# Layer 2 attention in steps of three score tiles, values twelve tiles behind

## The chip, the cores and the metric

The kernel runs on one core of a Trainium2 chip, in one launch. The metric is the device time of an execution in microseconds (us). The engines are TensorE (PE; its weight loads are listed as PEld), VectorE (DVE), ScalarE (ACT), GpSimd (POOL) and SyncE (SP), which only starts DMAs here. Each engine runs its own instructions in order, and they wait for each other on semaphores.

## The reference, cut to what matters

Four layers of cross attention and feed-forward, each different, are added to `x` [4, 256, 256] in turn. The change lies in the attention of layer 2: 16 query heads in 4 groups that share keys and values, 1601 context tokens and the 256 tokens of `x` itself (causal), root-mean-square norms on q and k, rotary positions on q and on the keys of `x`.

```python
q = rms_norm((x @ wq).reshape(B, L, 16, 128), q_norm_w)
k = rms_norm((x @ wk).reshape(B, L, 4, 128), k_norm_w)
v = (x @ wv).reshape(B, L, 4, 128)
k_ctx = rms_norm((h_ctx_kv @ wk_ctx).reshape(B, T, 4, 128), k_norm_w)
v_ctx = (h_ctx_kv @ wv_ctx).reshape(B, T, 4, 128)
q = q * cos + rotate_half(q) * sin
k = k * cos + rotate_half(k) * sin
k_full = jnp.repeat(jnp.concatenate([k_ctx, k], axis=1), 4, axis=2)
v_full = jnp.repeat(jnp.concatenate([v_ctx, v], axis=1), 4, axis=2)
scores = jnp.einsum('blhd,bmhd->bhlm', q, k_full) / np.sqrt(128) + mask
out = jnp.einsum('bhlm,bmhd->blhd', jax.nn.softmax(scores, axis=-1), v_full)
return out.reshape(B, L, 2048) @ wo
...
x = x + _L2_xattn_ref(_layernorm(x, axis=-1), ctx_2048, ...)
x = x + _L2_ffn_ref(_layernorm(x, axis=-1), ...)
```

## The kernel before

Everything is float32. The keys and values of the context were made in an earlier stage and lie in DRAM. `l2_xattn` (L1349 to L1725) goes through 16 *units*: 4 batches times 4 groups of heads. A unit has 4 heads, a head 4 *score tiles*, so there are 256 tiles in all. A tile covers 64 of the 256 queries and all keys.

What happens to a head, with the lines:

- `scores` (L1549): for each of its 4 tiles, 8 matmuls of 128 x 32 weights write a tile `s` of two PSUM banks (pool `ps_s`, 3 buffers). Four of them use four column groups of the array side by side. Each matmul in float32 leaves two records in the trace. VectorE adds the mask (L1564) and takes the maximum (`nmsm`, L1567), ACT takes the exponential into `p` with its sum (L1572). The four 32-row groups of a tile hold different keys, so maxima and sums are partial.
- `merge` (L1581): the partial maxima and sums are brought together: copies on POOL, `lo`, `em`, `wm`, `tot` on VectorE, one exponential on ACT, `rm` on POOL (L1600). It is a generator with one break in it, after the exponential.
- `scale` (L1607): POOL multiplies `p` by the shares, 8 instructions a head. `turn` (L1613): VectorE transposes `p` into `pT`, 6 instructions a head.
- `values` (L1618): 15 matmuls a head over 15 key tiles, in four chunks (`CHUNK`: 4, 4, 4, 3), add up in `o`, a pool of **one** PSUM buffer (`ps_o`). Behind the last, ACT copies `o` to `at` (L1627), which makes `o` free for the next head.
- `project` (L1629): once a unit, 8 matmuls with `wo` into `acc`, added to `x` by VectorE.

Beside it `prep` (L1452), a generator too, makes the q, k and v of the next unit in pieces: `turned` (L1401; once a batch: layernorm of `x` and its transposes `tp_ln`), two halves of q (`tpq`, L1470 to L1490, with the square on ACT `sqq` L1477 and `ss`, `qo`, `qt` on VectorE L1478, L1480, L1482), k and v (`tpkv`), norms and rotary positions, then transposes of q (`tpqT`, L1526, twice) and k (`tpk`, L1531). All these and `acc` share one PSUM buffer (tag "tp", pool `ps`). The layernorm of batches 1 to 3 takes its root from an activation table on ACT; `exps_next` brings the exponential's table back. `self.root` is a Newton iteration on VectorE instead.

The order of the instructions: the Python loop issues two score tiles at a time (8 steps a unit); between them go the softmax of the head before (`softmax_steps`) and the values of the head before that (`value_steps`, two chunks a step, 8 tiles behind their scores); `WHEN` and `BETWEEN` say in which steps a piece of `prep` is issued. A scheduler then orders each engine's instructions by itself. What goes through `self.pin` keeps its place. `self.mm` (L116) pins a matmul only when `self.strict` is set, which it is not here.

Of the kernel before, what the change touches and what calls it, by code (L numbers as in the profile page):

```python
# [11 lines left out]
F32 = mybir.dt.float32  # L12
# [85 lines left out]
class Kernel:  # L98
# [1262 lines left out]
    def l2_xattn(self):  # L1361
# [10 lines left out]
        with ExitStack() as es:  # L1372
# [28 lines left out]
            def turned(b):  # L1401

                xn = self.xn.tile([P, 2, D], F32, name="xn")
                if b:
                    self.layernorm(xn, self.x[b])
                    exps_next()
                else:

                    mv = self.small.tile([P, 2, 2], F32, name="ln_mv")
                    for q in range(2):  # L1410
                        st = self.small.tile([P, 6], F32, name="st3")
                        nc.vector.bn_stats(st, self.x[b][:, q, :])
                        nc.vector.bn_aggr(mv[:, q, :], st)
                    r = self.small.tile([P, 8], F32, name="ln_r8", bufs=1)
                    self.root(r[:, :2], mv[:, :, 1], 1.0, 1e-5, r[:, 2:])
                    for q in range(2):
                        nc.vector.tensor_scalar(
                            xn[:, q, :], self.x[b][:, q, :], mv[:, q, 0:1], r[:, q : q + 1],
                            ALU.subtract, ALU.mult,
                        )  # L1420
                    self.fill(LN2)
                tp = ps.tile([P, 2, 2, P], F32, name="tp_ln", tag="tp")
                for k in range(2):
                    for q in range(2):
                        nc.tensor.transpose(tp[:, k, q, :], xn[:, q, k * P : (k + 1) * P], self.ident)
# [26 lines left out]
            def prep(u, w, res):  # L1452
# [3 lines left out]
                va = two.tile([P, NK, HD2], F32, name="va2", bufs=3)  # L1456
                kT = two.tile([P, NK, P], F32, name="kT2")
                kd, vd = self.early_kv[u]
                for t, d in ((kT, kd), (va, vd)):
                    nc.sync.dma_start(t[:, :CT, :], d[:, :CT, :])  # L1460
                nc.sync.dma_start(kT[:, CT, :96], kd[:, CT, :96])
                nc.sync.dma_start(va[:96, CT, :], vd[:96, CT, :])
# [4 lines left out]
                kr = one.tile([P, 2, HD2], F32, name="kr2")  # L1467
                ss = self.small.tile([P, 2 + 8], F32, name="ss2")
                ra, rb = tabs["l2_qnw"]
                qo = []  # L1470
                for q in range(2):
# [17 lines left out]
                    yield  # L1489
# [11 lines left out]
                yield  # L1501
# [8 lines left out]
                nc.vector.tensor_reduce(ss[:, :2], sq, AX.X, ALU.add)  # L1510
                self.rstd(ss, ss, 1.0 / HD2, self.eps6)
# [18 lines left out]
                for m in range(2):  # L1530
                    nc.tensor.transpose(tp[:, m, :], ko[:, m, :], self.ident)  # L1531
# [17 lines left out]
            def scores(kT, qT, h, c, ms):  # L1549
# [10 lines left out]
                p = main.tile([P, 2, NK * 32], F32, name="p2", bufs=8)  # L1560
# [79 lines left out]
            def softmax_steps(hd):  # L1640


                shares = merge(hd["ms"])
                next(shares)
                yield
                r = yield from shares
                hd["pT"] = main.tile([P, 8, NK, 32], F32, name="pT2")
                for c in range(4):
                    scale(hd["p"][c], r, c)
                yield  # L1650
                for c in range(4):
                    turn(hd["p"][c], hd["pT"], c)
                yield

            def value_steps(hd):
                o = ps_o.tile([P, S], F32, name="o2")
                for n, ms in enumerate(CHUNK):
                    values(hd["va"], hd["pT"], hd["at"], hd["h"], o, ms)
                    if n % 2:
                        yield  # L1660
# [7 lines left out]
            for _ in self.early:  # L1668
                pass
# [818 lines left out]
```

## Time and profile before

| | |
|---|---|
| median of 3 runs | 2395.33 us (2391.05 to 2395.61) |
| the profiled execution | 2387.69 us |
| its span | 2386.0 us |
| granted TensorE clock, mean | 0.973 |
| busy in the span: PE, DVE, ACT, POOL | 2255.6, 1473.2, 1272.4, 948.7 us |
| attention of layer 2, first score matmul | 691.07 us |
| its last projection | 1686.51 us, 3.05 us long |

The span is the time between the first and the last instruction that the profiler recorded; the profiled execution's time is 1.7 us longer. In a list of groups, each line gives line of code, engine and operation, output and input tiles, size, count, then busy us and the mean ns of one, then the engine's idle time just before and what ended most of it. Some groups of this stage:

```profile
L1572 ACT ACTIVATE p<-s,nmsm 128x448 f32<-128x448 f32 (+2 forms) x512 | 324.7, 639 | 369.6 <-DVE nmsm L1567 317.4
L117 PE MATMUL o<-pT,va 128*128 128x256 f32 (+2 forms) x1920 | 431.7, 377 | 3.3 <-DVE pT L1613 2.9
L117 PE MATMUL s<-kT,qT 128*32 128x448 f32 (+2 forms) x4096 | 424.2, 550 | 4.2 <-ACT p L1572 4.2
L1607 POOL TENSOR_SCALAR p<-p,rm 128x448 f32<-128x448 f32 (+2 forms) x512 | 320.7, 649 | 6.3
L1567 DVE TENSOR_REDUCE nmsm<-s 128x1 f32<-128x448 f32 (+4 forms) x384 | 293.2, 783 | 4.4
L1613 DVE STREAM_TRANSPOSE pT<-p 128x448 f32<-128x448 f32 (+4 forms) x384 | 278.1, 778 | 11.1 <-POOL p L1607 11.1
```

PE's o and s hold 431.7 and 424.2 us of the stage's 998, and had to wait for 3.3 and 4.2 us. ACT's exponentials sat idle for 369.6 us before them, most of it until VectorE's maxima.

### The profile page before, as it was taken

To read this page: it belongs to the slowest core of one execution; us is meant where nothing else is said; L and a number is where in the kernel's file an instruction comes from. 1 tells how busy PE (TensorE), PEld (TensorE's weight loads), DVE (VectorE), ACT (ScalarE), POOL (GpSimd) and SP (SyncE) were. 2 spreads that over 40 slices of the span, in tenths; PEclk is the share of its full clock that TensorE was granted. 3 is DMA by queue.
4 is the path that set the end of the run, shared out by engine and by line. 5 is a ranking of instruction groups with operands and counts; after the bars stand their busy time and mean duration, and the time that the engine had idled before them with its cause. 6 is when DMAs were issued, how large, how long until landed. Compare 5 with 4: busy or idle time off the path is not lost.

```text
span 2386.0 us, 42230 instructions
## 1 busy us (share of the span) xinstructions
PE 2255.6 (95%) x14335; PEld 1382.2 (58%) x14335; DVE 1473.2 (62%) x3553; ACT 1272.4 (53%) x2877; POOL 948.7 (40%) x1707
## 2 busy tenths in 40 slices
PE   8989997889989999999999999999899889999996
PEld 5677875777745555555555655555665533444332
DVE  5453532773457777777777777777334574758344
ACT  3334443552474555555555555553232577888994
POOL 1014655503335544555554555554121253334220
PEclk9989998989999999999999999999899999999998
DMA  7165575652550111111111111100534353434320
GB/s 267 41 201 161 172 156 157 197 185 65 167 179 32 43 51 47 47 51 51 51 52 51 51 51 50 44 10 10 205 124 117 114 156 103 109 94 103 83 64 19
DMA packets 156078, 234.47 MB, mean 98 GB/s; under 512 B 33929, under 2 KB 122761, under 8 KB 154666
## 3 DMA queue, kind: packets, MB, share of 16 engines
q1 hardware_dynamic: 138998, 190.07, 25.0%
q0 software_dynamic: 11280, 31.60, 5.4%
q10 hardware_dynamic: 5588, 10.09, 1.4%
q8 instruction: 117, 1.92, 0.3%
q14 instruction: 95, 0.78, 0.1%
HBM read 169.94 MB, written 61.74 MB: 97 GB/s over the span
## 4 chain that ended last, share of the span: by engine, by line
PE 78%; DVE 7%; issue 5%; DMA 4%; ACT 2%; POOL 2%; SPq 1%; ACTq 0%; POOLq 0%; DVEq 0%
PE o L117 17%; PE s L117 17%; PE o L77 6%; PE b L77 3%; PE f2gu L117 3%; PE s L77 3%; PE f1gu L117 2%; PE fill L1307 2%; PE f0gu L117 2%; PE acc L117 2%; PE tpq L117 2%; PE av L117 2%; PE f0y L117 2%; PE f2y L117 1%; PE f1y L117 1%
## 5 line engine op out<-in xcount | busy, mean ns | idle before, releaser
L1572 ACT ACTIVATE p<-s,nmsm 128x448 f32<-128x448 f32 (+2 forms) x512 | 324.7, 639 | 369.6 <-DVE nmsm L1567 317.4
L117 PE MATMUL o<-pT,va 128*128 128x256 f32 (+2 forms) x1920 | 431.7, 377 | 3.3 <-DVE pT L1613 2.9
L117 PE MATMUL s<-kT,qT 128*32 128x448 f32 (+2 forms) x4096 | 424.2, 550 | 4.2 <-ACT p L1572 4.2
L77 ACT ACTIVATE e<-s 128x1024 f32<-128x1024 f32 (+1 forms) x416 | 392.4, 1041 | 57.4 <-PE s L77 56.3
L117 PEld LDWEIGHTS o<-pT,va 128*128 128x128 f32 (+1 forms) x1920 | 344.7, 190 | 127.9 <-issue 75.4
L1607 POOL TENSOR_SCALAR p<-p,rm 128x448 f32<-128x448 f32 (+2 forms) x512 | 320.7, 649 | 6.3
L1567 DVE TENSOR_REDUCE nmsm<-s 128x1 f32<-128x448 f32 (+4 forms) x384 | 293.2, 783 | 4.4
L1613 DVE STREAM_TRANSPOSE pT<-p 128x448 f32<-128x448 f32 (+4 forms) x384 | 278.1, 778 | 11.1 <-POOL p L1607 11.1
L117 PEld LDWEIGHTS s<-kT,qT 128*32 128x32 f32 x4096 | 121.7, 109 | 250.2 <-issue 213.9
L77 PE MATMUL o<-e,va 128*32 128x512 f32 x1656 | 246.9, 614 | 12.3 <-DVE os L77 12.2
L1600 POOL TENSOR_TENSOR rm<-em,tot 32x8 f32<-32x8 f32 x256 | 50.3, 197 | 335.6 <-DVE tot L1597 303.3
L1564 DVE TENSOR_TENSOR s<-s,mask 128x64 f32<-128x64 f32 (+4 forms) x384 | 92.5, 260 | 128.5 <-PE s L117 82.4
L77 PEld LDWEIGHTS s<-qb,kb 32*128 32x128 f32 (+1 forms) x1664 | 65.5, 180 | 182.3 <-issue 143.7
L1307 PE MATMUL fill<-wkc_early,ctxT 128*128 128x256 f32 (+1 forms) x444 | 110.5, 401 | 8.9 <-ACT va_early L1315 6.7
L522 POOL DMA_INDIRECT f0xr<-f0xd,f0src x95 | 91.3, 961 | 66.5 <-PE f0y L117 25.5
L77 PE MATMUL s<-qb,kb 32*128 32x256 f32 (+1 forms) x1664 | 111.5, 331 | 3.1 <-ACT e L77 1.8
L77 POOL CAST kb<-kf 128x384 fp32r<-128x384 f32 (+1 forms) x126 | 65.5, 549 | 96.4 <-PE s L77 61.8
L1307 PEld LDWEIGHTS fill<-wkc_early,ctxT 128*128 128x128 f32 (+1 forms) x444 | 87.0, 200 | 25.3 <-ACT va_early L1315 7.8
L1572 ACT ACTIVATION_READ_ACCUMULATOR p<-s,nmsm 128x1 f32 x512 | 100.5, 196 | 0.0
L1326 DVE TENSOR_REDUCE ss_early<-sq_early 128x4 f32<-128x512 f32 x64 | 37.1, 580 | 82.8 <-ACT sq_early L1325 72.0
L630 POOL DMA_INDIRECT f0yt<-f0yd,f0slot x64 | 63.1, 987 | 60.7 <-DVE x L622 29.8
L117 PE MATMUL f2gu<-f2wgu,f2xsT 128*128 x176 | 85.1, 608 | 0.6 <-ACT f2xsT L114 0.3
(579 smaller groups left out, 3689.2 us busy)
## 6 DMA issues: line engine op xcount, KB each, us to landing
kf<-kd SPq DMA_DIRECT2D x384, 48.0 KB
vd<-va_early SPq DMA_DIRECT2D x96, 128.0 KB
kd<-kT_early SPq DMA_DIRECT2D x48, 256.0 KB
kT<-kd SPq DMA_DIRECT2D x16, 768.0 KB
va<-vd SPq DMA_DIRECT2D x16, 768.0 KB
kd<-kt SPq DMA_DIRECT2D x96, 128.0 KB
f0yd<-f0ys SPq DMA_DIRECT2D x95, 128.0 KB
ctxT<-in_ctxT SPq DMA_DIRECT2D x5, 1664.0 KB
```

What stands on the lines that cost most here:

```text
L77: ins = f(*a, **kw)
L117: self.ordered(self.nc.tensor.matmul(out, lhsT, rhs, start=start, stop=stop, **kw))
L522: nc.gpsimd.indirect_dma_start(out=t, out_offset=None, in_=xd[:, :], in_offset=bass.IndirectOffsetOnAxis(ap=src[:, n : n + 1], axis=0),)
L630: nc.gpsimd.indirect_dma_start(out=yt, out_offset=None, in_=yd[:, :], in_offset=bass.IndirectOffsetOnAxis(ap=slot[:, t, r : r + 1], axis=0),)
L1307: ins = nc.tensor.matmul(tp[:rows, t, :], ctxT[u // NKV2][:, k, c0 : c0 + rows], w[u % NKV2][:, k, :], start=k == 0, stop=k == 1,)
L1326: nc.vector.tensor_reduce(ss[:, m0:m1], sq[:, : m1 - m0, :], AX.X, ALU.add)
L1564: nc.vector.tensor_tensor(sv, sv, mask[:, e0:e1, : nt - CT, :].rearrange("p n t i -> p n (t i)"), ALU.add)
L1567: nc.vector.tensor_reduce(ms[:, 0, e0:e1], s[:, n0:n1, : nt * 32], AX.X, ALU.max, negate=True)
L1572: nc.scalar.activation(p[:, n, : nt * 32], s[:, n, : nt * 32], AF.Exp, bias=ms[:, 0, e : e + 1], accum_out=ms[:, 1, e : e + 1],)
L1600: nc.gpsimd.tensor_tensor(r[32 * a : 32 * a + 32], e[:, a], tot, ALU.mult)
L1607: nc.gpsimd.tensor_scalar(p[:, n, : nt * 32], p[:, n, : nt * 32], r[:, e : e + 1], 1.0, ALU.mult, ALU.mult)
L1613: self.pin(nc.vector.transpose(pT[:, 2 * c + n0 : 2 * c + n1, :nt, :].rearrange("p n t i -> p n (t i)"), p[:, n0:n1, : nt * 32],))
```

## The change

Tiles are numbered through all units: tile x belongs to head x // 4, to unit x // 16, and has place k = x % 16 in it.

- A step has three score tiles, issued one after the other, instead of two (`scores` returns `s`; mask, maximum and exponential are in `weights`, which is issued by `soften`).
- Values run `LATE` = 12 tiles behind: in the step of tiles x to x + 2, chunks of the tiles x - 12 to x - 10 (one chunk a tile).
- A head's merge and scaling come one step after its last tile, its transposes another step later. The ring of `p` has 12 buffers instead of 8.
- `self.strict` is set over the loop, and the transposes on PE go through `ordered`: PE runs the matmuls in the order in which they are written.
- `beside` places the pieces of `prep`, the loads and the projection by k. A unit's first pieces are made two units ahead of it. In `prep` the order is now: first half of q; loads of k and v, and `tpkv`; second half of q; norms.
- The layernorm in `turned` takes Newton's root for every batch.

```diff
@@ -1401,28 +1401,23 @@
             def turned(b):
...
-                if b:
-                    self.layernorm(xn, self.x[b])
-                    exps_next()
-                else:
...
+                r = self.small.tile([P, 8], F32, name="ln_r8", bufs=1)
+                self.root(r[:, :2], mv[:, :, 1], 1.0, 1e-5, r[:, 2:])
+                if b == 0:
                     self.fill(LN2)
...
-                        nc.tensor.transpose(tp[:, k, q, :], xn[:, q, k * P : (k + 1) * P], self.ident)
+                        self.ordered(nc.tensor.transpose(tp[:, k, q, :], xn[:, q, k * P : (k + 1) * P], self.ident))
@@ -1453,22 +1448,15 @@
-                va = two.tile([P, NK, HD2], F32, name="va2", bufs=3)
-                kT = two.tile([P, NK, P], F32, name="kT2")
-                kd, vd = self.early_kv[u]
-                for t, d in ((kT, kd), (va, vd)):
-                    nc.sync.dma_start(t[:, :CT, :], d[:, :CT, :])
-                nc.sync.dma_start(kT[:, CT, :96], kd[:, CT, :96])
-                nc.sync.dma_start(va[:96, CT, :], vd[:96, CT, :])
                 if u % NKV2 == 0:
                     self.xb = turned(b)
                     yield
                 xb = self.xb
-                kr = one.tile([P, 2, HD2], F32, name="kr2")
                 ss = self.small.tile([P, 2 + 8], F32, name="ss2")
-                ra, rb = tabs["l2_qnw"]
                 qo = []
-                for q in range(2):
+                def query(q):
+                    ra, rb = tabs["l2_qnw"]
...
-                    yield
+                query(0)
+                yield
+                va = two.tile([P, NK, HD2], F32, name="va2", bufs=3)
+                kT = two.tile([P, NK, P], F32, name="kT2")
+                kd, vd = self.early_kv[u]
+                for t, d in ((kT, kd), (va, vd)):
+                    nc.sync.dma_start(t[:, :CT, :], d[:, :CT, :])
+                nc.sync.dma_start(kT[:, CT, :96], kd[:, CT, :96])
+                nc.sync.dma_start(va[:96, CT, :], vd[:96, CT, :])
+                kr = one.tile([P, 2, HD2], F32, name="kr2")
                 tp = ps.tile([P, 2, 256], F32, name="tpkv", tag="tp")
...
-                yield
...
                 sq = one.tile([P, 2, HD2], F32, name="sq2")
                 nc.scalar.activation(sq, kr, AF.Square)
                 nc.vector.tensor_reduce(ss[:, :2], sq, AX.X, ALU.add)
+                yield
+                query(1)
+                yield
                 self.rstd(ss, ss, 1.0 / HD2, self.eps6)
                 exps_next()
...
-                    nc.tensor.transpose(tp[:, m, :], ko[:, m, :], self.ident)
+                    self.ordered(nc.tensor.transpose(tp[:, m, :], ko[:, m, :], self.ident))
...
-            def scores(kT, qT, h, c, ms):
...
-                p = main.tile([P, 2, NK * 32], F32, name="p2", bufs=8)
+                return s
+            def weights(s, c, ms):
+                p = main.tile([P, 2, NK * 32], F32, name="p2", bufs=12)
                 for n0, n1, nt in spans(c):
...
+            def value_chunk(hd, n):
+                if n == 0:
+                    hd["o"] = ps_o.tile([P, S], F32, name="o2")
+                values(hd["va"], hd["pT"], hd["at"], hd["h"], hd["o"], CHUNK[n])
 
             units = [(b, g) for b in range(B) for g in range(NKV2)]
             w = load(0)
             wo = load_out(0)
+            results = {0: []}
+            for n, _ in enumerate(prep(0, w, results[0])):
                 self.fill(Q2 if n == 0 else C2 if n == 3 else 0)
             for _ in self.early:
                 pass
+            w = load(1)
             self.es2.close()
             main = es.enter_context(tc.tile_pool(name="a2main", bufs=2, side="right", reuse_waits="tile"))
 
 
+            heads, pieces = [], {}
+            def begin(n):
+                for _ in pieces[n] if n else ():
+                    pass
+                kT, va, qT = results[n]
                 at = main.tile([P, 4, S], F32, name="at2", bufs=2)
                 for h in range(4):
+                    heads.append({"kT": kT, "va": va, "qT": qT, "at": at, "h": h, "b": units[n][0], "wo": wo, "p": []})
+            def prepare(n):
+                if n < len(units):
+                    if n not in pieces:
+                        pieces[n] = prep(n, w, results.setdefault(n, []))
+                    next(pieces[n], None)
+            def beside(n, k):
+                nonlocal w, wo
+                if k == 11 and n:
+                    project(heads[4 * n - 1])
+                if k in (1, 3, 7, 9) or (n, k) == (0, 0):
+                    prepare(n + 1)
+                if k == 12:
+                    for _ in range(2):
+                        prepare(n + 1)
+                    if n + 1 < len(units):
+                        wo = load_out(units[n + 1][1])
+                if k == 3 and n + 2 < len(units):
+                    w = load(units[n + 2][1])
+                if k == 15 or (k == 13 and (n + 2) % NKV2 == 0):
+                    prepare(n + 2)
+            def turns(hd):
+                hd["pT"] = main.tile([P, 8, NK, 32], F32, name="pT2")
+                for c in range(4):
+                    turn(hd["p"][c], hd["pT"], c)
+            def soften(made):
+                for hd, c, s in made:
+                    hd["p"].append(weights(s, c, hd["ms"]))
+            self.strict = True
+            merging, turning = [], []
+            LATE, ALL = 12, 16 * len(units)
+            for x0 in range(0, ALL + LATE, 3):
+                made, norms = [], False
+                for x in range(x0, min(x0 + 3, ALL)):
+                    if x % 16 == 0:
+                        begin(x // 16)
+                    hd = heads[x // 4]
+                    if x % 4 == 0:
+                        hd["ms"] = self.small.tile([P, 2, 8], F32, name="nmsm2")
+                    made.append((hd, x % 4, scores(hd["kT"], hd["qT"], hd["h"], x % 4)))
+                soften(made[:1])
+                merges = [(hd, merge(hd["ms"])) for hd in merging]
+                for _, steps in merges:
+                    next(steps)
+                soften(made[1:2])
+                for hd, steps in merges:
+                    try:
+                        next(steps)
+                    except StopIteration as end:
+                        for c in range(4):
+                            scale(hd["p"][c], end.value, c)
+                for pos in range(3):
+                    x = x0 + pos
+                    if LATE <= x < ALL + LATE:
+                        value_chunk(heads[(x - LATE) // 4], (x - LATE) % 4)
+                    if pos == 0:
+                        soften(made[2:])
+                    if x < ALL:
+                        beside(x // 16, x % 16)
+                        norms |= x % 16 == 4
+                    if pos == 0:
+                        for hd in turning:
+                            turns(hd)
+                if norms:
+                    prepare(x0 // 16 + 1)
+                turning, merging = merging, [hd for hd, c, _ in made if c == 3]
+            project(heads[-1])
+            self.strict = False
```

The old loop, which the new one replaces, is in the functions printed above (`softmax_steps`, `value_steps`, `WHEN`, `BETWEEN`).

## Prediction

> **What bounds the kernel now.** First the page's busy time and chain, to see which engine and which stage.
>
> ```profile
> PE 2255.6 (95%) x14335; PEld 1382.2 (58%) x14335; DVE 1473.2 (62%) x3553; ACT 1272.4 (53%) x2877; POOL 948.7 (40%) x1707
> ...
> PE 78%; DVE 7%; issue 5%; DMA 4%; ACT 2%; POOL 2%; SPq 1%; ACTq 0%; POOLq 0%; DVEq 0%
> PE o L117 17%; PE s L117 17%; PE o L77 6%; PE b L77 3%; PE f2gu L117 3%; PE s L77 3%; PE f1gu L117 2%; PE fill L1307 2%; PE f0gu L117 2%; PE acc L117 2%; PE tpq L117 2%; PE av L117 2%; PE f0y L117 2%; PE f2y L117 1%; PE f1y L117 1%
> ```
>
> TensorE sets the end, and the two largest entries (s and o, L117, 17% each) are the stage that is changed. Its first score matmul starts at 691.07 us and its last projection ends near 1689.6. Three windows of that stage (start and end, length, then busy us with instructions of PE, PEld, DVE, ACT, POOL, then granted clock, DMA share, GB/s) and PE's waits in it:
>
> ```profile
> 700.00:720.00 20.00, 15.78 (x121) 5.35 (x113) 17.68 (x41) 15.03 (x41) 10.60 (x24) 0.91 0.09 33
> 719.00:1659.00 940.00, 939.22 (x6348) 550.32 (x6348) 727.18 (x1577) 487.62 (x1359) 483.80 (x1076) 1.00 0.13 44
> 1660.00:1680.00 20.00, 17.66 (x96) 12.95 (x94) 13.85 (x27) 4.17 (x14) 12.33 (x28) 1.00 0.00 0
> ```
>
> ```profile
> PE s L117 <- ACT p L1572: 4.2, 3, 2.6
> PE o L117 <- DVE pT L1613: 0.3, 1, 0.3
> ```
>
> PE is busy for 939.22 of 940 us at full clock: nothing is waited for, so only what PE itself spends can be saved there. The waits lie in the start (4.2) and the end. Busy is not useful, though. A timeline of PE around two changes of kind (start, length, records of each run) shows it:
>
> ```profile
> 1016.93 0.99 PE L117 MATMUL s<-kT,qT 128*32 128x480 f32 x8
> ...
> 1017.33 0.59 PE L117 MATMUL s<-kT,qT 128*32 128x480 f32 x4
> 1017.84 0.48 PE L117 MATMUL o<-pT,va 128*128 128x256 f32 x1
> ...
> 1018.16 0.59 PE L117 MATMUL o<-pT,va 128*128 128x256 f32 x2
> ...
> 1039.71 0.27 PE L1526 MATMUL tpqT<-ident,qo 128*128 128x128 f32 x1
> 1040.02 0.48 PE L117 MATMUL o<-pT,va 128*128 128x256 f32 x1
> ```
>
> Four score records go side by side, a set every 0.40 us (1016.93 to 1017.33). From the last set to the first value record it is 1017.84 less 1017.35 (start of the set's fourth record) = 0.496 where the records of a set take 0.382 from there to the next set: +0.114. That first record lasts until 1018.16, 0.320, where later ones are 0.216 apart: +0.104. Into a score run, 0.309 follows the last record instead of 0.216, +0.094, and the first set is 0.024 longer. One score run costs 0.336 us of turnover. From transposes to values it is 0.306 instead of 0.109 (1039.71 to 1040.02) and again 0.104: 0.301. From values to q products, k/v products, projection or transposes it is nothing.
>
> **The change part by part.** *Steps of three tiles.* In the issue order of the two builds PE has 126 score runs before and 86 after. Before: 126 entries x 0.118, 111 exits to values x 0.218, 15 exits to q transposes x (0.114 + 0.060), 15 times transposes to values x 0.301: 14.9 + 24.2 + 2.6 + 4.5 = 46.2. After: 86 x 0.118 + 86 x 0.218 + 30 transposes to values x 0.301 (the pieces now stand among values, not before scores): 10.1 + 18.7 + 9.0 = 37.9. **-8.3 us**. The 38 joints from q, k/v and projection products to values do not occur before; nearest is values to the same products, 0, at most the transposes' 0.301: 0 to 11. I take 0, since shape and width are those of values.
>
> One rule speaks against this gain: the Trainium skill, "TensorE: Matmul & The Clock Gate", Part 2, says that PE loads weights ahead of matmuls in flight. By that a change of kind would be free and this term 0, the total 8.3 later; the 0.496 and 0.320 above differ, and the rows decide.
>
> *PE's order is pinned, values twelve tiles behind.* PSUM has one bank for o. The last chunk of a head must be copied (L1627) before the next head's first value matmul. Before, the two were parted: the copy ended 0.82 to 0.93 after the last record's start and the next head began 2.55 to 5.55 later still. After, the two chunks follow in one step if the last falls on its position 0 or 1, with only a piece between: q products (1.72 us), projection (1.3 before it needs that copy), or, at the unit's tile 7, four transposes (0.64). The bare copy:
>
> ```profile
> 1680.22 6.45 PE L117 MATMUL o<-pT,va 128*128 128x256 f32 x30 [2.54 <-DVE pT L1613]
> 1686.51 3.05 PE L117 MATMUL acc<-wo,at 128*128 128x256 f32 x12
> ...
> 1686.71 0.37 ACT L1627 COPY at<-o 128x256 f32<-128x256 f32 x1 [9.48 <-PE o L117]
> ```
>
> Uncovered it costs 0.379 (a record) + 0.04 + 0.37 - 0.216 = 0.57. Tile 7's 0.64 would hide just that, but ACT is in order, and in the built order that copy stands behind an exponential of the same step's tiles, which needs VectorE's maximum. A step is some 9.8 us of PE (3 x 1.65 scores, 22.5 x 0.216 values), 10.5 to 13.4 with a piece. VectorE averages 727.18 / 940 = 77%, but is uneven: six transposes (4.3 us) fall in one step with a query half (ss 0.69, qo 0.68, qt 0.68) that waits for ACT's square (0.60). By these rows I walked the 16 steps that repeat every three units:
> - Units 3, 6, 9, 12 (tile 7 at position 1): VectorE's transposes end 3.8 us into the step, the copy's exponentials follow, the copy ends 9.5 to 9.9 in; PE wants the bank at 8.65. 1.3 us each, times 4: 5.2.
> - Units 2, 5, 8, 11, 14 (position 0): behind the k sum of squares, three transposes and the query half, the copy ends 8.3 to 8.7 in, wanted at 6.85. 1.9 us each, times 5: 9.5.
> - Elsewhere the walk leaves 0.3 us or more.
> **+14.7**. Bounds: 0 if VectorE is 1.9 us earlier than walked; 9 x 3.0 = 27, where 3.0 is its fullest step, 12.8, less 9.8. I take the walk. Queued behind the waiting PE are only its own values and next scores; the wait gives VectorE time, so nothing is late after it.
> The last unit has no pieces: five bare handoffs x 0.6, **+3.0** (2.1 to 4.7).
>
> *Start and end.* The 2.54 idle before 1680.22 was VectorE's last turns. After, head 63's chain of merge, scaling and turns is some 16.2 us against 17.3 of values still to do: **-2.5** (0 to -2.5). At the start the first values come after 15 tiles instead of about 11 and fewer pieces fill PE: idle 4 to 6 instead of 4.2, and a q product (1.72) that stood in it moves out: **+1** (-4 to +5).
>
> *At no cost.* Newton roots for batches 1 to 3: fewer ACT table loads, some ten small VectorE operations each; PE waited for neither before, and the result is wanted a step later. If VectorE has no slack there, some 1.5 us three times. The k and v loads go behind a query, some 15 tiles (50 us) ahead of use, at 0.13 DMA share; the query weights a unit ahead. SP's order behind them stays. The larger weights ring (8 to 12) only takes waits away.
>
> **Sum.** -8.3 + 14.7 + 3.0 - 2.5 + 1 = +7.9. On the profiled execution's 2387.69 that is 2395.6; the median of the runs is 2395.33, 7.6 above it, so I forecast the median + 7.9 = **2403**.
>
> **The rivals.** *The cover holds (faster):* the copies come before PE wants the bank, at tile 7 of nine units. For it: VectorE idles 23% on average, and one us of walk error clears half. Against: in order it cannot use that idle time early. Decides when the copy ends within 6.85 and 8.65 us of the step's start: -8.3 + 3.0 - 2.5 + 1 = -6.8, 2388.5; with no bare handoffs either 2385.5.
> *Half of it:* one of the two kinds of unit stalls: -6.8 + 5.2 or 9.5, 2394 to 2398, not told from before.
> *The throttle joins:* after the start's idle 2.60 us the clock in the first window was 0.91: (1 - 0.91) x 20 = 1.8 us lost; after 2.54 idle in the third it stayed 1.00. If each of nine stalls were followed by that: 9 x 1.8 = 16, 2419. Against it, each stall is shorter than either.
> The same page's Part 1 gives an idle window of about 3.4 us before the clock is halved; by it this rival is 0, though 2.60 us was enough (with 0.91 and 0.70 shortly before) in the first window.
> *Scores wait for their buffers:* three tiles fill the ring of three; a tile's exponential has about 4.9 us of values as cover. If VectorE's uneven steps break that too, +0.5 us in 30 steps, 2418.
>
> **How the numbers follow.** Forecast 0.42 (its own range 2397 to 2412, mostly the stalls' 8 to 24), cover holds 0.25, half 0.15, throttle or buffers 0.18. This kernel's times differ by 0.2% between runs, so same is 2390.5 to 2400.1. Faster: 0.25. Same: the half and the forecast's lowest 0.05, 0.20. Slower: 0.37 + 0.18 = 0.55. The range leaves out a tenth at each end: 2385 to 2421.
>
> **What would show it.** Right: PE busy falls by some 8 us in the middle windows at clock 1.00, and PE o waits for ACT's at copy 14 times, some 18 us in sum, the nine at tile 7 the longest; the idle before the tail's values is gone. Wrong: waits at those nine absent (cover holds); score waits on p (buffers); clock under 1.00 after stalls; or a last set to first value record no longer 0.496, or products to values not 0.216.

## The result and the profile after

The changed kernel takes 2412.55 us (median of 4 runs, 2410.57 to 2415.17), the kernel before 2395.40 (4 runs): a ratio of 1.0077, with a 95% interval of 1.0059 to 1.0094. That is 17 us slower. Its profiled execution took 2415.17 us, its span is 2413.5.

Busy time of the engines on the page, and the stage in three windows (start and end; length; busy us of PE, PEld, DVE, ACT, POOL with instructions; granted clock, DMA share, GB/s). The windows go from the first score matmul to tile 48, from there to tile 192, and on to the last projection. The kernel before, cut at the same tiles:

```profile
691.00:867.00 176.00, 171.70 (x1175) 94.97 (x1174) 135.41 (x293) 95.95 (x267) 89.71 (x201) 0.99 0.14 50
867.00:1427.00 560.00, 559.39 (x3780) 328.27 (x3782) 433.98 (x941) 294.15 (x812) 288.72 (x639) 1.00 0.14 49
1427.00:1690.00 263.00, 259.87 (x1722) 155.84 (x1714) 193.74 (x420) 123.08 (x345) 128.10 (x288) 1.00 0.08 28
```

And the changed kernel:

```profile
PE 2249.5 (93%) x14322; PEld 1389.0 (58%) x14335; DVE 1506.1 (62%) x3586; ACT 1267.4 (53%) x2871; POOL 950.4 (39%) x1707
...
701.00:887.00 186.00, 170.31 (x1157) 92.44 (x1156) 138.85 (x293) 95.95 (x267) 90.51 (x197) 0.97 0.16 53
887.00:1448.00 561.00, 552.19 (x3772) 330.25 (x3770) 445.12 (x937) 290.98 (x809) 290.54 (x640) 1.00 0.15 49
1448.00:1713.00 265.00, 259.85 (x1749) 160.76 (x1748) 202.45 (x425) 122.23 (x346) 129.53 (x293) 1.00 0.08 26
```

PE's busy time fell by 6 us over the span, and by 7.2 in the middle window (559.39 to 552.19), where the kernel before was idle for only 0.6 us: the longer runs do save work. But the middle window is no shorter, and the first is 10 us longer. To the hundredth, from the times of the tiles' first score records: the first 48 tiles take 186.35 us instead of 176.14, the next 144 take 560.61 instead of 559.46, and the stage, to the start of the last projection's last record, 1011.75 instead of 998.12. PE's waits in the stage of the changed kernel (total, times, longest):

```profile
PE o L117 <- ACT at L1631: 13.0, 15, 1.6
PE tpkv L117 <- issue: 5.2, 2, 4.3
PE acc L117 <- ACT at L1631: 3.2, 4, 0.8
PE s L117 <- ACT p L1576: 2.6, 3, 1.4
PE tpqT L1526 <- POOL qo L1516: 2.4, 1, 2.4
PE tpk L1531 <- DVE x L1639: 1.9, 1, 1.9
PE o L117 <- DVE pT L1617: 1.0, 1, 1.0
```

Three things stand here.

*The single o bank.* Of the 15 waits for the copy, five are at tile 7 in position 0 (1.19 to 1.58 us), four at tile 7 in position 1 (0.81 each), five are the bare ones of the last unit (0.46 to 0.52), one is in the start. Timelines of VectorE, ACT and PE of the changed kernel, in this order, at one of the first kind show why (start, length, engine, line, tiles, records):

```profile
1039.35 3.19 DVE L1617 STREAM_TRANSPOSE pT<-p 128x896 f32<-128x896 f32 x4
1042.48 0.42 DVE L1568 TENSOR_TENSOR s<-s,mask 128x192 f32<-128x192 f32 x2
```

```profile
1044.09 0.66 ACT L1576 ACTIVATE p<-s,nmsm 128x480 f32<-128x480 f32 x1 [5.08 <-DVE nmsm L1571]
...
1044.74 0.65 ACT L1576 ACTIVATE p<-s,nmsm 128x480 f32<-128x480 f32 x1
...
1045.38 0.60 ACT L1576 ACTIVATE p<-s,nmsm 128x416 f32<-128x416 f32 x1
...
1045.96 0.38 ACT L1631 COPY at<-o 128x256 f32<-128x256 f32 x1
```

```profile
1042.81 1.56 PE L117 MATMUL o<-pT,va 128*128 128x256 f32 x6
1044.20 0.60 PE L1526 MATMUL tpqT<-ident,qo 128*128 128x128 f32 x4
1046.38 0.48 PE L117 MATMUL o<-pT,va 128*128 128x256 f32 x1 [1.58 <-ACT at L1631]
```

The last chunk is done near 1044.4, and ACT has been idle for 5.08 us just before. But VectorE was at its transposes until 1042.48 and its masks and maxima come after; the exponentials wait for these, and the copy stands behind three of them.

*The start.* Timelines of PE and of VectorE of the changed kernel:

```profile
706.72 1.98 PE L117 MATMUL tpq<-wq,xT 128*128 128x512 f32 x4
713.01 3.38 PE L117 MATMUL tpkv<-wks,xT 128*128 128x256 f32 x8 [4.30 <-issue]
```

```profile
710.46 0.66 DVE L1571 TENSOR_REDUCE nmsm<-s 128x1 f32<-128x480 f32 x1
711.04 0.67 DVE L1466 TENSOR_REDUCE ss<-sqq 128x4 f32<-128x512 f32 x1
711.63 0.68 DVE L1468 TENSOR_TENSOR qo<-tpq,l_qnwra 128x512 f32<-128x512 f32 x1
712.23 0.68 DVE L1470 TENSOR_TENSOR qt<-tpq,l_qnwrb 128x512 f32<-128x512 f32 x1
```

The k and v products need the buffer that the query half has just filled. The view names no releaser, but by the times VectorE reads that buffer last: it does so only after the masks and maxima of three tiles, until 712.9, and PE, in pinned order, may not take the next scores meanwhile.

*Before the stage.* The first score matmul comes 74.9 us after the start of the last expert matmul of the layer before it (626.2 to 701.06), where it was 71.5 (619.5 to 691.07). The experiments find the reason.

### The profile page after: what moved, and what is told of

The parts are those of the page before. It is cut to its first block, busy times and chain, and to the rows that moved or that the text cites. A ratio compares the mean times of both kernels' runs of the same rounds, so it can differ in the third digit from the quotient of the medians.

```text
span 2413.5 us, 42181 instructions
## 1 busy us (share of the span) xinstructions
PE 2249.5 (93%) x14322; PEld 1389.0 (58%) x14335; DVE 1506.1 (62%) x3586; ACT 1267.4 (53%) x2871; POOL 950.4 (39%) x1707
## 4 chain that ended last, share of the span: by engine, by line
PE 65%; DVE 18%; ACT 6%; issue 6%; DMA 2%; POOL 2%; SPq 0%; another core or an unknown queue 0%; ACTq 0%; PEld 0%; POOLq 0%; DVEq 0%; PEldq 0%
PE o L117 11%; PE s L117 10%; PE o L77 7%; DVE pT L1617 4%; PE b L77 3%; DVE nmsm L1571 3%; PE f2gu L117 3%; ACT p L1576 3%; PE s L77 3%; PE f1gu L117 2%; PE f0gu L117 2%; PE fill L1307 2%; PE acc L117 2%; PE av L117 2%; PE f0y L117 2%
## 5 line engine op out<-in xcount | busy, mean ns | idle before, releaser
L117 PE MATMUL s<-kT,qT 128*32 128x448 f32 (+2 forms) x4096 | 414.3, 552 | 2.6 <-ACT p L1576 2.6
L1571 DVE TENSOR_REDUCE nmsm<-s 128x1 f32<-128x448 f32 (+4 forms) x384 | 298.8, 785 | 7.4 <-DVE s L1568 0.2
L77 PE MATMUL o<-e,va 128*32 128x512 f32 x1656 | 248.0, 617 | 14.1 <-DVE os L77 12.2
L1326 DVE TENSOR_REDUCE ss_early<-sq_early 128x4 f32<-128x512 f32 x64 | 37.2, 581 | 85.0 <-ACT sq_early L1325 65.4
```

The costliest lines, as they stand in the source:

```text
L77: ins = f(*a, **kw)
L117: self.ordered(self.nc.tensor.matmul(out, lhsT, rhs, start=start, stop=stop, **kw))
L1326: nc.vector.tensor_reduce(ss[:, m0:m1], sq[:, : m1 - m0, :], AX.X, ALU.add)
L1571: nc.vector.tensor_reduce(ms[:, 0, e0:e1], s[:, n0:n1, : nt * 32], AX.X, ALU.max, negate=True)
```

## The experiments

The stage is counted from the first score matmul to the start of the last projection record in the run's profile, the stretch before it from the start of the last expert matmul of layer 1. "The 48 tiles" and "the steady tiles" are the first 48 score tiles and the 144 behind them, as in the windows above. The first four kernels ran on a chip on which the kernel before took 2343.0; ratios compare. The intervals are 95%. Stage and stretch come from one profiled execution each. Behind the stage the code is the same in all kernels, and yet these executions take from 695.0 us (e3) to 703.5 (e6) there, so a median need not show all of a gain in the stage.

| kernel | median us | before | ratio | stage us | stretch before |
|---|---|---|---|---|---|
| before (profile shown) | | | | 998.1 | 71.5 |
| changed kernel (profile shown) | 2412.55 | 2395.40 | 1.0077 (1.0059 to 1.0094) | 1011.8 | 74.9 |
| e1 two halves of the bank | 2364.37 | 2343.03 | 1.0081 (1.0053 to 1.0109) | 1013.6 | 73.6 |
| e2 steps of two | 2352.97 | 2343.03 | 1.0046 (1.0032 to 1.0059) | 1000.8 | 72.8 |
| e3 first loads early | 2364.72 | 2343.03 | 1.0087 (1.0059 to 1.0116) | 1015.0 | 72.9 |
| e4 start's pieces spread | 2360.77 | 2343.03 | 1.0075 (1.0052 to 1.0098) | 1007.6 | 74.2 |
| e5 changed kernel again | 2414.06 | 2395.32 | 1.0070 (1.0048 to 1.0093) | 1015.4 | 75.8 |
| e6 copy first | 2404.14 | 2395.32 | 1.0040 (1.0026 to 1.0053) | 1002.0 | 75.5 |
| e7 pieces moved | 2412.64 | 2395.32 | 1.0061 (1.0038 to 1.0084) | 1007.2 | 76.7 |
| e8 PE order free | 2401.64 | 2395.32 | 1.0027 (1.0014 to 1.0039) | 1003.9 | 74.3 |
| e9 steps of three, repaired | 2395.85 | 2395.07 | 1.0009 (0.9997 to 1.0021) | 999.4 | 77.6 |
| e10 steps of two, repaired | 2403.44 | 2395.07 | 1.0038 (1.0024 to 1.0052) | 1006.5 | 76.3 |
| e11 before with Newton's roots | 2402.08 | 2395.07 | 1.0025 (1.0015 to 1.0036) | 1000.6 | 76.6 |
| e12 steps of three, roots as before | 2395.68 | 2395.88 | 0.9996 (0.9985 to 1.0007) | 997.5 | 71.8 |

**e1, two halves of one bank for o.**

```diff
-                    hd["o"] = ps_o.tile([P, S], F32, name="o2")
+                    hd["o"] = oo[:, hd["h"] % 2, :]
...
+            oo = ps_o.tile([P, 2, S], F32, name="o2")
```

> Theory (the single o bank costs): heads take turns in two halves of one bank, so no first value matmul waits for ACT's copy of the head before. The trace of the changed kernel has 15 such waits with 13.0 us of idle, and each also loses about 0.16 (a record's length beyond its spacing) and 0.10 (slow first record): 13.0 + 15 x 0.26 = 17. Two of the 15 may return as waits for the turned weights. Expected 2396 to 2400. Rival (VectorE is late, the copy only comes last): the same places then wait for pT or p, the gain is under 4, 2409 or more. Second rival: writing one half of a bank while ACT reads the other slows the values, slower than 2413.

The profile still has 15 waits for the copy, 14.1 us: in the built program a head's first value matmul still waits for the copy of the head before, although they use different halves. So the run did not take the wait away: why the built program keeps it is not shown, neither rival is decided, and what a second bank would bring stays open. The run is the changed kernel once more.

**e2, steps of two tiles.**

```diff
-            for x0 in range(0, ALL + LATE, 3):
+            for x0 in range(0, ALL + LATE, 2):
```

(The two inner ranges follow.)

> Only the step is two tiles again, with everything else of the change kept. Score runs go from 86 to 126. Theory (a score run costs 0.336 us): +13.4. But every head's last chunk then closes a step, so that two tiles of scores cover each copy: the 15 waits, 17 us, go. Sum about -4, 2409. Rival (a change of kind is free, as weights are loaded ahead): only the waits go, 2396. If the waits stay, 2412 to 2426.

Measured 1.0046, with 3 waits for the copy, 1.9 us. In the 144 steady tiles it takes 556.7 us, where e1, e3 and e4 on the same chip take 562.1 to 562.5: 5.4 to 5.8 less. By the sum, 24 more score runs x 0.336 = 8.1 were paid, and e1's waits there, some 13.0 (10.0 of idle in the profile, and about 0.27 for each of 11 restarts, worked out in the last section), saved: -4.9. If a change of kind were free, it would have been 13. So both the waits and the price of a score run hold in the steady part, to within 1 us. The gain in the whole, 11.4 us beside e1, is larger than the 4 us expected, mostly because the start is better too: 180.7 us for 48 tiles instead of 185.6 (e1) and 187.4 (e3).

**e3, the first unit's loads early.**

```diff
+                if u == 0:
...
+                    nc.sync.dma_start(kT[:, CT, :96], kd[:, CT, :96])
+                    nc.sync.dma_start(va[:96, CT, :], vd[:96, CT, :])
                 if u % NKV2 == 0:
                     self.xb = turned(b)
```

> For the first unit alone, keys and values are loaded before its layernorm again, as before the change. Theory: from the layernorm's transposes to the first score matmul 40.4 us passed after the change and 37.5 before, because the loads now stand behind the first query half on SP; 2.9 us come back, 2409.6. Rival (those 2.9 us are chance, as the first 640 us differ by 6 us between the two profiles where the code is the same): 2412.5.

2364.72 beside e1's 2364.37 on the same chip: nothing came back, and from the layernorm's transposes to the first score matmul it still takes 40.1 us. The loads are not the cause. But it was not chance either: in every run of this study with Newton's roots it is 39.9 us or more, where the kernel before has 37.1.

**e4, the start's pieces spread.**

```diff
-                if k in (1, 3, 7, 9) or (n, k) == (0, 0):
+                if k in ((1, 3, 7, 9) if n else (0, 3, 6, 10, 11)):
...
-                        norms |= x % 16 == 4
+                        norms |= x == 8 if x < 16 else x % 16 == 4
```

> For the first unit alone, the next unit's pieces stand at tiles 0, 3, 6, 8, 10, 11 instead of 0, 1, 3, 5, 7, 9. Theory (PE's fixed order makes the k and v products wait 4.30 us for the buffer of the query half just before them, and the query transposes 2.35 us for POOL): these two waits go, most of the 11.7 us idle of the first 18 tiles with them, -5 to -8, 2405 to 2408. Rival (the start is bound by VectorE's and ACT's first softmax, and the idle only moves to the scores' waits for p): -1 or less, 2411 or more.

The wait of the k and v products is gone, but the query transposes now wait 5.1 us for POOL instead of 2.4. The first 48 tiles take 179.6 us instead of 186 to 187, the time is 3.6 to 4.0 below e1 and e3 on the same chip: less than the 5 to 8 expected. The theory holds for the one wait; the other only grew.

**e5, the changed kernel again,** as a control on the chip of e6 to e8.

> The changed kernel unchanged, to stand beside the others of this group on one chip. Expected: 0.77% over the kernel before, 0.6 to 0.95; its attention stage, from the first score matmul to the last projection, 1010 to 1016 us, with 15 waits of values for the copy, 13 to 14 us.

As expected: 1.0070, a stage of 1015.4 us, 15 waits of 14.1.

**e6, copy first.** Exponentials and copies are pinned on ACT, and chunks that end a head are issued earlier:

```diff
+                last = x0 % 4
+                if last == 3 and LATE <= x0 < ALL + LATE:
+                    value_chunk(heads[(x0 - LATE) // 4], 3)
                 soften(made[:1])
...
-                    if pos == 0:
+                    if pos == (last == 2):
                         soften(made[2:])
```

> The copies of o and the exponentials are put in a fixed order on ACT: the copy of a head's last chunk stands ahead of all exponentials of its step where that chunk has position 0, and ahead of the third tile's where it has position 1. PE's order is that of the changed kernel. Theory (the copies stand behind exponentials that wait for VectorE): waits of values for the copy fall from 13 to 14 us to under 5 (the five bare ones of the last unit and some tenths), 10 to 12 us less than the changed kernel with the restarts. Rival (the bank would be waited for anyway, since the exponentials now come later and the scores wait for their buffers): the same time, or waits of s for p of about the same sum.

9.9 us less than the control. The two largest entries of PE's waits in this run:

```profile
PE o L117 <- ACT at L1631: 8.0, 9, 1.4
PE s L117 <- ACT p L1576: 5.5, 3, 2.6
```

All five waits at position 0 are gone, so the copy's place in ACT's order made them, not VectorE as such. The four at position 1 rose from 0.81 to 1.43, as the second tile's exponentials are pinned ahead of the copy there. So these waits are 8.0 us and not under 5. The rival's waits for p are three, ahead of the tiles numbered 9, 11 and 13. Of the 13.4 us by which the stage is shorter than the control's, 8.5 lie in the first 48 tiles (178.9 instead of 187.4) and only 3.8 in the 144 steady ones (558.7 instead of 562.5). In the first 48 PE waits 11.8 us instead of 15.7 and the granted clock is 0.985 instead of 0.964; two of the gone waits for the copy, 2.2 us, are among them. So the right number is in large part owed to the start, of which the theory had not spoken.

**e7, pieces moved.**

```diff
-                if k in (1, 3, 7, 9) or (n, k) == (0, 0):
+                if k in ((3, 7, 10, 12) if n else (0, 1, 3, 7, 9)):
...
-                        norms |= x % 16 == 4
+                        norms |= x % 16 == (8 if x > 15 else 4)
```

> From the second unit on, the pieces move: k and v products to tile 3, the second query half to tile 7, norms to the step of tile 8, query transposes to 10 and 12, key transposes to 13. So 1.72 us of products instead of 0.64 us of transposes stand between the two chunks at tile 7. Theory (cover decides): the nine waits at tile 7, 10.0 us in the trace of the changed kernel, shrink by 1.1 us each or to nothing, 8 us less in all with the restarts, if the query half's chain does not come too late for the transposes. Rival: a query half's three VectorE instructions are what makes VectorE late; the waits only move with it to the next handoff, at tile 11, and the time stays within 3 us.

The longer cover does shorten the waits for the copy, from 14.1 us to 3.4, and the stage is 8.2 us shorter than the control's (1007.2 to 1015.4): 6.0 in the 144 steady tiles, 2.3 behind them, nothing in the start. That is the theory's 8. But the median is only 1.4 below the control, within the interval. In the two profiled executions, 1.2 us apart, the rest lies outside the stage: it begins 2.4 us later, and what follows it takes 4.5 us longer. So in the stage the theory holds, and the time of the whole does not tell it from the rival. Two other waits are new, the first and the fourth of the list:

```profile
PE acc L117 <- ACT qT L1527: 9.0, 5, 1.8
...
PE tp_ln L1420 <- ACT kT L1534: 3.7, 3, 2.2
```

The projection now stands right behind a query transpose and waits for the one tp buffer. Neither side had this: where the o bank is no longer waited for, the other single bank is, and the 8.2 us are what is left of the gain.

**e8, PE's order free.**

```diff
-            self.strict = True
             merging, turning = [], []
```

> PE's order is not pinned; steps of three, twelve tiles behind, pieces and roots stay. The scheduler then cuts the 86 score runs into 101 and moves chunks apart. Theory (the pinned order makes the waits): the start and the handoffs recover, 10 to 20 us less than the changed kernel, less 15 x 0.336 = 5: about level with the kernel before, ratio 0.998 to 1.005. Rival (the waits come from what stands where on VectorE and ACT, whatever PE's order): within 4 us of the changed kernel.

12.4 us less than the control. The first 48 tiles take 176.3 us, as in the kernel before; the next 144 take 562.0, as in the control (562.5). So the pinned order costs some 11 us in the start, and none in the steady part: there PE waits 4.7 us instead of 9.8 and makes 54 score runs instead of 48, 2.0 us at 0.336 each; the other 2.8 us that PE is busy longer are not explained.

**e9, steps of three with three repairs:** e6, the copy ahead at position 1 too, e4's idea with the transposes later, and the first unit's pieces in the old order.

```diff
+                if last == 2:
+                    for x in (x0, x0 + 1):
+                        if LATE <= x < ALL + LATE:
+                            value_chunk(heads[(x - LATE) // 4], (x - LATE) % 4)
                 soften(made[1:2])
...
+                if k in ((1, 3, 7, 9) if n else (0, 3, 6, 13, 14)):
...
                 query(0)
                 yield
+                if u == 0:
+                    query(1)
+                    yield
```

> Steps of three with three repairs. ACT: as in the copy-first run, and where the last chunk has position 1 its copy stands ahead of the second tile's exponentials too. Start: the next unit's pieces stand at tiles 0, 3, 6, 8, 13, 14 of the first unit. Before the loop: the first unit makes both query halves and then k and v, as before the change. Theory (handoffs, start and the first unit's order are what was lost; 40 fewer score runs are worth what 48 tiles in steady state showed): stage 1015.4 in the control, less 13.4 (copy-first), less 4 x 1.4 for position 1, less 6 for the start, 990; and 3 to 4 from the first unit's order between the layernorm's transposes and the first score matmul (41 to 37). 2384 to 2390 where the control had 2414, ratio to before 0.995 to 0.998. Rival (VectorE sets the pace of three-tile steps, so what is taken from one wait comes back at scores): stage 998 or more, ratio over 1.000.

1.0009: level with the kernel before, not ahead of it. The steady part went as foreseen (555.6 us for 144 tiles, 3.1 below e6, with the waits at position 1 down to 0.15). The start did not: 180.7 us for 48 tiles, 1.8 above e6. And the old order of the first unit did not bring back the stretch before the stage. By its numbers (stage 998 or more, ratio over 1.000) the rival came true, the ratio within the noise; but waits of scores for p, its mechanism, stand in the first 48 tiles alone, 7.6 us, and none in the steady ones.

**e10, steps of two** with the last two repairs.

> Steps of two with the repairs of the start and of the first unit's order (ACT free, as no handoff falls inside a step). Theory: stage 1000.8 less 6 to 8 for the start, 993 to 995, first unit's order 3: ratio 1.0046 less 10 / 2350 = 1.000 to 1.001, and 1 to 5 us above the three-tile kernel beside it, since 40 score runs x 0.336 = 13.4 stand against what is left of its handoffs (five bare ones, four projections, 6 to 8 us). Rival (runs of three are worth nothing): as fast as the three-tile kernel or faster.

7.6 us above e9. The start got worse (186.4 us), with waits for p of up to 5.3 us and a key transpose waiting 3.7; this spacing of pieces does not suit steps of two. Most of the difference is this start, 5.7 us. In the 144 steady tiles steps of two are 0.9 us slower than e9 (556.5 to 555.6): 24 score runs x 0.336 = 8.1, against 3.5 us of waits and some 3 of restarts that e9 still has there and e10 has not. So the runs of three keep their price, but little of it is left as gain.

**e11, the kernel before with Newton's roots,** that is the first hunk of the change alone (the transposes aside).

> The kernel before with the Newton root for batches 1 to 3 alone. Theory (off TensorE's path): within 1.5 us of the kernel before; the first score matmul to the last projection 997 to 999. Rival: the table loads that go, about 1.3 us each, twice a batch, stood on the path: 3 x 2.6 = 8 us faster; or VectorE's small operations stand on it: 2 to 5 us slower.

7.0 us slower, and the interval excludes zero. Steady tiles are as in the kernel before (559.2 us for 144, 559.5 there). What is late is mostly the first unit: the stretch before the stage is 76.6 instead of 71.5. Timelines of VectorE in this kernel, in the kernel before, and in e12, in this order:

```profile
674.84 0.16 DVE L145 SCALAR_TENSOR_TENSOR ln_r<-ln_r 128x2 f32<-128x2 f32 x1
675.11 0.41 DVE L1412 TENSOR_SCALAR xn<-x,ln_mv,ln_r 128x256 f32<-128x256 f32 x1
675.44 0.68 DVE L1473 TENSOR_REDUCE ss<-sqq 128x4 f32<-128x512 f32 x1
```

```profile
664.03 0.17 DVE L126 RECIPROCAL ln_rs<-ln_rs 128x2 f32<-128x2 f32 x1 [0.94 <-ACT ln_rs L125]
665.03 0.69 DVE L1478 TENSOR_REDUCE ss<-sqq 128x4 f32<-128x512 f32 x1 [0.83 <-ACT sqq L1477]
```

```profile
671.20 0.17 DVE L126 RECIPROCAL ln_rs<-ln_rs 128x2 f32<-128x2 f32 x1 [0.80 <-ACT ln_rs L125]
672.65 0.69 DVE L1471 TENSOR_REDUCE ss<-sqq 128x4 f32<-128x512 f32 x1 [1.28 <-ACT sqq L1470]
```

The scheduler does not leave the roots of batches 1 to 3 where the code calls for them, 200 us later and more: it puts them among the first unit's query half. Each is a chain of twelve small instructions, 0.1 to 1.2 us apart. Those of batches 1 and 2 stand ahead of the sum of squares, the second from 669.26 to the line shown at 674.84; that of batch 3 follows, from 677.67, so it is two and not three that come first. In the kernel before the sum of squares starts 2.55 us after the start of its query product (662.48 to 665.03), here 8.4 (667.03 to 675.44), in the changed kernel 8.4 as well (667.25 to 675.65).

**e12, e9 without the new start, and with roots from ACT's table for batches 1 to 3.**

> Steps of three with ACT's fixed order as in the run of three repairs, the first unit's order of before, the pieces of the start as in the change, and the layernorms of batches 1 to 3 with the root from ACT's table as before. Theory (the scheduler puts the three Newton chains, some 30 small instructions, on VectorE ahead of the first unit's query half, which then starts near 675 us instead of 665): the stretch from the layernorm's transposes to the first score matmul goes from 41 to 43 back to 37 or 38, and the time is 6 us under the run of three repairs, as the kernel before was 6 under itself with Newton's roots; 1 or 2 more because the start of the copy-first run was 1.7 better: ratio to before 0.996 to 0.998. Rival (the 6 us of the Newton run were chance of that build): that stretch stays over 40 us and the ratio is 1.000 or more.

The stretch from the transposes to the first score matmul is 37.2 us, as in the kernel before, the sum of squares starts 2.56 us after its product, and the stage takes 997.5. That settles where the roots cost: the rival is out. The time does not follow in full: 0.9996 against e9's 1.0009, some 3 us where 6 were expected, and the intervals overlap. This kernel is as fast as the one before and not faster. Its waits:

```profile
PE s L117 <- ACT p L1585: 5.7, 3, 2.6
PE tpkv L117 <- issue: 3.7, 6, 2.6
PE o L117 <- ACT at L1640: 2.9, 9, 0.5
PE acc L117 <- ACT at L1640: 2.0, 4, 0.5
PE tpk L1540 <- DVE x L1648: 2.0, 1, 2.0
```

It is 4.2 us ahead over the 144 steady tiles (555.3 to 559.5) and 3.1 behind over the first 48 (179.3 to 176.1). The 4.2 are not all owed to runs of three: steps of two in e2 and e10, with the same delay of values and pinned order, take 556.5 to 556.7, so some 3 us of it come without them. What was not tried: a free order for the first tiles together with the repairs, and the delay of twelve by itself.

## Why the prediction was right or wrong

The direction was right, and 2412.55 lies in the range, but in good part by luck. The size was not right: +17.2 where +7.9 was forecast, just outside the forecast's own 2397 to 2412. The reason given for a slower kernel was that the handoffs (+14.7) cost more than the score runs save (-8.3). Both effects are there, but in the 144 steady tiles they nearly cancel, +1.15. What makes the kernel slower is mostly the start (+10.2) and the roots (some +3.3), which stood in the sum at +1 and at nothing; the end of the stage gives the other +2.3.

- *Fewer score runs, -8.3.* Too small. The charge of 0.301 for transposes followed by values was no price of the switch but a wait for VectorE, which the view of PE counts as busy. In the kernel before, 14 of 15 such joints show it, each ahead of a head's first value matmul, and at all 14 VectorE's last transpose of that head ends 0.05 us before that matmul starts. The 15th has only 0.110 from transpose to value, and there VectorE was done 0.31 us before it (value at 732.48). VectorE of the kernel before ahead of the joint at 1040.02 that the prediction shows, and ahead of the 15th:

```profile
1038.78 1.18 DVE L1613 STREAM_TRANSPOSE pT<-p 128x960 f32<-128x960 f32 x1 [0.34 <-POOL p L1607]
```

```profile
730.99 1.18 DVE L1613 STREAM_TRANSPOSE pT<-p 128x960 f32<-128x960 f32 x1 [0.22 <-POOL p L1607]
```

  In the changed kernel all ten joints from key transposes to values and nine of those from query transposes show none. Two narrow windows of PE's timeline of the changed kernel:

```profile
748.46 0.27 PE L1531 MATMUL tpk<-ident,ko 128*128 128x128 f32 x1
...
748.68 0.38 PE L117 MATMUL o<-pT,va 128*128 128x256 f32 x1
```

  (The second transpose starts at 748.57, the value record 0.109 later, which is the transposes' own spacing.) Without that charge on the changed kernel, 30 x 0.301 = 9.0, the term is -17.3. Over the 144 steady tiles it makes 24 x 0.336 + 9 x 0.30 = 10.8, which with 11.5 of waits (8.8 of idle, ten restarts of 0.27) gives +0.7; measured +1.15. The 0.336 for a score run stands. By the prediction's reading of the rule that weights are loaded ahead, a change to or from score matmuls would have been free; it was not. The joints from products to values cost nothing, as taken.
- *Handoffs at tile 7, +14.7.* The mechanism, the nine places and the two kinds were right, and e6 shows that ACT's order is what decides. The walk was somewhat late: 1.19 to 1.58 instead of 1.9, 0.81 instead of 1.3, together 10.0 of idle, some 12.4 with 0.27 for each restart. (One row was misread on the way: in the kernel before nearly all copies end 1.20 to 1.31 us after the last record's start; 0.82 to 0.93 is where they begin. The 2.55 to 5.55 behind them are right, so nothing in the sum hangs on it.) The rival in which the cover holds is excluded, since none of the nine was hidden.
- *Bare handoffs of the last unit, +3.0.* Five, 0.46 to 0.52 idle, 2.4 in sum, some 3.7 with the restarts. The end's 2.54 of idle is gone, as taken.
- *Elsewhere 0.3 us or more is left.* Wrong in places: the projection waited 0.8 us for its fourth copy four times (its 1.3 us of cover was not enough behind ACT's exponentials), and once a key transpose waited 1.95 us for the tp buffer, behind VectorE's addition, followed by 3.4 us at half clock.
- *The start, +1, bounded at +5.* This term failed. The first 48 tiles take 10.2 us more, although four tiles' values, 6.5 us (7.5 records of 0.216 each), come later. PE waits there for 15.7 us instead of 4.2, and the clock is 0.97 instead of 0.99. The prediction had 4 to 6 us of idle: it left out that pinned, PE cannot take the scores behind a product or transpose that has to wait, as in the 4.30 and 2.4 us shown above. e8 shows it: without the pin the 48 tiles take 176.3 where the control takes 187.4.
- *Newton's roots, nothing.* Wrong. I asked whether PE waited for the layernorms of batches 1 to 3 where the code has them, not where the scheduler puts them. Alone they cost 7.0 us (e11). In the changed kernel the stretch before the stage grew by 3.3 us (4.3 in the control).
- *The throttle.* It came in the start and after the one 1.95 us wait, not after the nine.

The stage's +13.6 and the stretch's +3.3 make 16.9 of the 17.2; that it comes so near is chance, since in the control they make 21.6 where the medians are 18.7 apart. (The two profiled executions are 27.5 us apart. The other 10.6 lie earlier than the stretch, 6.7, and behind the stage, 3.9, where the code is the same; executions of the kernel before spread over nearly 15 us on one chip.)

## What to carry to other kernels

A pinned order can turn an uneven moment of another engine into a wait. Here it cost some 11 us in the first 48 tiles and nothing in the 144 behind them: cost the start by itself. When a single buffer is handed on, look at what stands ahead of the emptying instruction in its engine's queue, not at that engine's idle share. And a small constant between two kinds of matmul need not be the price of the change: look whether another engine's instruction ends just before it. An edit that looks free because its result is wanted late has to be looked up in the built order: a scheduler may run it early, ahead of something that is on the path.

## What the runs showed of the hardware

After an idle PE of about 2 us the clock may or may not be halved: of eight runs with a wait of 1.91 to 2.04 us for the tp buffer at this one place, five show half clock for 3.4 us right behind it, and three do not. Windows right behind a 1.95 us wait in the changed kernel, and behind a 2.01 us wait at the same place in e12 (the clock is the third number from the end):

```profile
873.00:878.00 5.00, 4.51 (x30) 1.43 (x34) 2.35 (x4) 0.37 (x1) 0.17 (x1) 0.66 0.01 2
```

```profile
866.00:871.00 5.00, 5.00 (x50) 1.62 (x47) 3.83 (x10) 2.16 (x7) 0.12 (x1) 1.00 0.01 3
```

Waits of up to 1.8 us never had that effect in the stage of these fourteen profiles. So the idle window of about 3.4 us that the prediction cites was no safe bound here. And a value matmul that had to wait loses more than its idle time: from the last transpose to it 1.852 us pass in the case shown above, where 0.109 is the spacing without a wait, and its own record takes 0.320 instead of 0.218. With 1.58 us of idle in the profile that is 0.27 more.
